# A decoder layer whose opening loads are reordered: part of the weights is fetched behind the first batch's opening, and SyncE and DVE take over loading work from GpSimd

## The chip, the cores and the metric

The kernel runs on one core of one Trainium2 chip. Its time is the device time of one execution in microseconds; lower is better. Kernels are compared by the median of several runs. One execution is taken with the hardware profiler, and all traces below come from such executions.

The core has five engines, each with a program of its own that it executes in order: TensorE (PE; its weight loads are listed apart as PEld), VectorE (DVE), ScalarE (ACT), GpSimd (POOL) and SyncE (SP). They wait for each other by semaphores. Transfers between the chip's main memory and the on-chip memory (SBUF) are issued by an engine's queue, here SyncE's and GpSimd's, and carried out by 16 DMA engines that all queues share. Matmul results are written to PSUM, whose buffers are few.

## The reference

One post-norm decoder layer in float32, batch 4, 1024 tokens of 256 features, a context of 154 tokens:

```python
x = _layernorm(x + self_attention(x))
x = _layernorm(x + cross_attention(x, ctx, distances))
x = _layernorm(x + mixture_of_experts(x))
```

The self attention has three parts. The first has 16 heads of 16 features, and its scores are scaled by a gate before the softmax:

```python
mod = sigmoid(x @ cg_W + cg_b + (cons_vec @ am_W + am_b))
scores = (q @ k.T / sqrt(16)) * mod[..., None]
```

Two further attentions of 4 heads of 64 features follow ("causal" on `x`, "meta" on the mix of the two), each mixed in by a constant weight, and an output projection. The cross attention adds `-log(distances + 1e-9) * abs(distance_scaling)` to its scores, where `distances` is 4 x 1024 x 154. The last part routes each token to 2 of 8 experts and adds a shared expert.

## The kernel before

**Stages.** Tokens lie on 128 partitions, 8 tiles of 128 to a batch. The four batches run one after the other through both attentions; then all 4096 tokens are routed, sent to their experts through a table in main memory (`scratch`), and put together again. `scratch` has 9216 rows of 258 numbers and is filled with zeros and with default row numbers at the start of the kernel by two transfers, `scratch<-empty` (9.4 MB) and `scratch<-rows` (9216 pieces of 8 bytes), lines 255 to 261. It is used again only after the attentions.

**The opening of a batch** is the generator `begin(b)`. It transposes the tokens on PE (`xT`, copied out by ACT), projects the gate (`project_mod`: PE, a Tanh on ACT, an affine step on POOL), `q` (PE, then DVE, which needs the gate and the bias `bq`) and `k` (PE, then ACT, which needs `bk`). Then come 12 steps of `maxima` (the lead): PE computes a 128 x 1024 block of scores (L422) into one of two large PSUM buffers, and DVE takes its maxima (L429). Between them lie the value projections of the first attention (L302, then DVE L310), and behind them the 8 tiles of the causal attention's values. For batches 1 to 3 `begin` runs step by step inside the batch before; for batch 0 it runs alone at the start.

**The main loop** has 128 steps for each batch. A step does one `maxima`, 12 steps ahead, and one `exponentials`: PE makes a block of scores (L460) into small PSUM buffers (three, and one accumulator), and ACT turns each half into exponentials (L471). Every fourth step's exponentials are multiplied with the values (L480). At steps 4, 8 and 12 the gate, `q` and `k` of the next group of heads are projected (L288).

**Loads.** The weights are loaded before `begin(0)` in the order of the text. `load_plain` issues one transfer from SyncE. `load_head_cols` loads a 256 x 256 matrix into a staging tile by SyncE; POOL fills a wider tile with zeros and copies the 16 heads' columns into it, at a distance of 32. `load_head_bias` issues four tiny transfers from POOL into a tile that DVE has filled; `load_cols` and `load_bcast` issue one each from POOL. The staging tiles share ten buffers (tag `ex`) with the exponentials, and `empty` and `rows` share theirs with later tiles of the tags `avq` and `rb`.

**What sets the order.** The text is written in one sequence. A scheduler distributes it over the engines and may place an instruction earlier or later in an engine's program where data allow; what it placed is what each engine executes. So the logarithm over `bias` (the distances of a batch, line 942: ACT, then a multiply by `nds` on DVE, line 943), written far behind the main loop, stands among the first instructions of ACT and DVE for batch 0. `nds` is the negated scaling, loaded at line 248 and finished by two small DVE operations (L250, L251). `cabout` and `mcbout` are biases that DVE scales after they are loaded (L230).

SyncE's transfers use eight semaphores in turn, and so do POOL's: an issue waits until the transfer issued eight places before it on the same engine has landed.

The transfers of `bias` and `cn` (the context) of a batch are issued at the head of the batch's loop (lines 816 and 818), for batch 0 just ahead of `begin(0)` and, in the order of SyncE's queue, ahead of the two fills of `scratch`.

Of the kernel before, what the change touches and what calls it, by code (L numbers as in the profile page):

```python
# [8 lines left out]
F32 = mybir.dt.float32  # L9
# [31 lines left out]
def run(gen):  # L41
    for _ in gen:
        pass
# [3 lines left out]
def decoder_layer(ctx: ExitStack, tc: tile.TileContext, a, out):  # L47
# [85 lines left out]
    with tc.tile_pool(name="wA", bufs=1) as wA, tc.tile_pool(name="work", bufs=2) as work:  # L133


        def load_plain(name, src, n):
            t = wA.tile([P, src.shape[0] // P, n], F32, tag=name, name=name)
            nc.sync.dma_start(t, src.rearrange("(c p) n -> p c n", p=P))
            return t

        def load_head_cols(name, src):

            st = work.tile([P, NC2, H], F32, tag="ex", name="stage", bufs=EXB)
            nc.sync.dma_start(st, src.rearrange("(c p) n -> p c n", p=P))
            t = wA.tile([P, NC2, NH, 32], F32, tag=name, name=name)
            nc.gpsimd.memset(t, 0.0)
            for c in range(NC2):
                nc.gpsimd.tensor_copy(
                    t[:, c, :, 0:HD], st[:, c, :].rearrange("p (h d) -> p h d", d=HD)
                )  # L150
            return t.rearrange("p c h w -> p c (h w)")

        def load_head_bias(name, src, extra):

            t = wA.tile([P, NG], F32, tag=name, name=name)
            if extra == 0.0:
                nc.vector.memset(t, 0.0)
            else:
                tmp = work.tile([P, NG], F32, tag="tmpb", name="tmpb")
                nc.vector.memset(tmp, extra)  # L160
                nc.vector.tensor_scalar(t, tmp, rowmx, None, ALU.mult)
            v = src.rearrange("(g j d) -> j d g", j=4, d=HD)
            for j in range(4):
                nc.gpsimd.dma_start(t[32 * j : 32 * j + HD, :], v[j])
            return t

        def load_cols(name, src):
            t = wA.tile([P, src.shape[0] // P], F32, tag=name, name=name)
            nc.gpsimd.dma_start(t, src.rearrange("(c p) -> p c", p=P))
            return t  # L170

        def load_bcast(name, src):
            t = wA.tile([P, H], F32, tag=name, name=name)
            nc.gpsimd.dma_start(t, src.unsqueeze(0).to_broadcast([P, H]))
            return t


# [60 lines left out]
        xwq = load_head_cols("xwq", a["xWqT"])  # L238
        xbq = load_head_bias("xbq", a["L0_xattn_bq"], 0.0)
        xwk = load_head_cols("xwk", a["xWkT"])  # L240
        xbk = load_head_bias("xbk", a["L0_xattn_bk"], 0.0)
        xwv = load_plain("xwv", a["xWvT"], H)
        xbv = load_bcast("xbv", a["L0_xattn_bv"])
        xwo = load_plain("xwo", a["xWoT"], H)
        xbo = load_bcast("xbo", a["L0_xattn_bo"])

        nds = wA.tile([P, 1], F32, tag="nds", name="nds")
        nc.gpsimd.dma_start(nds, a["ds"].to_broadcast([P, 1]))
        nds2 = work.tile([P, 1], F32, tag="nds2", name="nds2", bufs=1)
        nc.vector.tensor_scalar(nds2, nds, -1.0, None, ALU.mult)  # L250
        nc.vector.tensor_tensor(nds, nds, nds2, ALU.min)  # L251


        empty = work.tile([P, H], F32, tag="avq", name="empty", bufs=3)
        nc.gpsimd.memset(empty, 0.0)
        rows = work.tile([P, TILES, 2], F32, tag="rb", name="rows", bufs=1)
        nc.gpsimd.memset(rows, 0.0)
        iota(rows[:, :, 0], [[P, TILES]], 2 * B * S, 1)
        sv = scratch.rearrange("(t p) w -> p t w", p=P)
        nc.sync.dma_start(sv[:, :, 0:H], empty.unsqueeze(1).to_broadcast([P, TILES, H]))  # L260
        nc.sync.dma_start(sv[:, :, H:RW], rows)


        def ex_tile(shape, name):
# [512 lines left out]
        def end(b, cx4):  # L777
# [28 lines left out]
            if b < B - 2:  # L806

                nc.sync.dma_start(kept[b].rearrange("(t p) d -> p t d", p=P), y)
                load_y(b + 2)

        behind = iter(())
        for b in range(B):
            y = ys[b]
# [525 lines left out]
```

## Time and profile before

| | us |
|---|---|
| median of 6 runs | 3434.39 |
| lowest and highest run | 3430.82 and 3438.36 |
| the profiled execution | 3439.73 |
| its span (first to last instruction) | 3437.9 |

The mean granted clock of TensorE in the profiled execution was 0.974 of full speed.

The profile's rows read as follows. In the timeline: start in us from the beginning of the span, duration, engine, line of the kernel, operation, `output<-input` by the program's names, shapes, count (x), and in brackets the idle time of the engine just before and what ended it. "SPq" is an issue by SyncE's queue: its duration is that of the issue, not of the transfer. A float32 matmul of the program appears as two rows. In the table of stretches each row holds the busy time of the five engines, the number of instructions, the granted clock of PE (1.00 is full speed), the share of the DMA engines in use and what they moved.

Some durations of the opening that are used below:

| what | us |
|---|---|
| projection of 128 x 1024 (L288, 8 rows) at full clock | 3.60 to 3.70 for 8 rows, 4 matmuls |
| one DVE maximum (L429) | 1.22 to 1.24 |
| one lead step of scores and values at half clock | 4.02 |
| 16 value matmuls of the causal attention (L302, 32 rows) | 8.69 |
| exponentials of half a block (L471) | 0.60 |
| ACT's Ln over `bias` (L942) | 1.32 |
| ACT's table load | 1.28 |
| SyncE issues at the start, from one to the next | 0.49 to 0.62 |

### The profile page before, as it was taken

The numbers are of one execution on the slowest core, as the hardware profiler recorded it, in microseconds if no ns is written. First come the engines' busy times: TensorE is split into PE (matmuls) and PEld (weight loads), VectorE is DVE, ScalarE is ACT, GpSimd is POOL, SyncE is SP. The second block draws the span as 40 slices with busy tenths as digits, with TensorE's granted clock in tenths as the row PEclk, the third lists the DMA queues.
The fourth block names the chain that finished last, engine by engine and source line by source line (L and its number), as shares of the span: only waits on it lengthen the run. The fifth ranks groups of instructions, "written<-read, shape, count | busy, mean of one in ns | idle before, by whom it ended". The sixth has DMA issues, their size and how long they took to land.

```text
span 3437.9 us, 60936 instructions
## 1 busy us (share of the span) xinstructions
PE 3305.1 (96%) x25260; PEld 2086.4 (61%) x25260; DVE 1725.6 (50%) x3571; ACT 1600.8 (47%) x3130; POOL 373.4 (11%) x601
## 2 busy tenths in 40 slices
PE   7999999999999999999999999999999999999997
PEld 4555667566556675665566656555667665555554
DVE  3565555565655555656555556565556541122224
ACT  1555545375555344755564447555544731222223
POOL 4000000000000000000000000000000018212123
PEclk7999999999999999999999999999999999999999
DMA  9000000000000000000000000000000052111114
GB/s 203 1 2 1 1 1 1 3 21 14 1 1 1 1 1 3 21 13 2 1 1 1 1 3 9 1 2 1 1 1 1 1 204 82 44 44 44 44 44 156
DMA packets 75866, 84.13 MB, mean 24 GB/s; under 512 B 15136, under 2 KB 65928, under 8 KB 75592
## 3 DMA queue, kind: packets, MB, share of 16 engines
q1 hardware_dynamic: 68040, 61.53, 6.6%
q0 software_dynamic: 7552, 18.70, 1.6%
q8 instruction: 202, 3.31, 0.4%
q14 instruction: 72, 0.59, 0.1%
HBM read 46.52 MB, written 33.69 MB: 23 GB/s over the span
## 4 chain that ended last, share of the span: by engine, by line
PE 81%; DVE 9%; POOL 3%; issue 3%; ACT 2%; DMA 2%; SPq 0%; ACTq 0%; DVEq 0%; POOLq 0%
PE big L288 10%; PE big L422 8%; PE big L530 8%; PE one L566 7%; PE acc L584 7%; PE big L1226 7%; PE one L480 7%; DVE mxp L429 6%; PE one L460 4%; PE acc L1248 4%; PE one L697 3%; PE big L662 3%; PE one L302 2%; PE acc L716 2%; PE big L630 2%
## 5 line engine op out<-in xcount | busy, mean ns | idle before, releaser
L429 DVE TENSOR_REDUCE mxp<-big 128x2 f32<-128x1024 f32 x512 | 610.5, 1219 | 304.9 <-PE acc L460 252.2
L422 PE MATMUL big<-k,q 31*128 31x512 f32 x2048 | 596.0, 644 | 30.3 <-DVE mxp L429 26.7
L471 ACT ACTIVATE ex<-one 128x512 f32<-128x512 f32 x696 | 391.3, 601 | 248.5 <-PE acc L460 184.3
L460 PE MATMUL one<-q,k 32*128 32x256 f32 x2784 | 502.0, 397 | 0.0
L269 DVE CUSTOM_DVE_ANT_0 prob<-big,zero_t 128x1024 f32<-128x1024 f32 x256 | 303.6, 1222 | 270.8 <-PE big L530 270.6
L460 PEld LDWEIGHTS one<-q,k 32*128 32x128 f32 x2784 | 326.9, 185 | 31.1 <-ACT ex L471 2.5
L549 ACT ACTIVATE prob<-prob,nmx 128x1024 f32<-128x1024 f32 x256 | 293.0, 1153 | 22.2 <-DVE nmx L269 21.6
L530 PE MATMUL big<-mk,mq 64*128 64x512 f32 x1024 | 283.0, 630 | 2.4 <-ACT ex L468 2.4
L422 PEld LDWEIGHTS big<-k,q 31*128 31x128 f32 x2048 | 179.9, 189 | 172.1 <-DVE mxp L429 93.7
L571 ACT COPY pt<-one 128x512 f32<-128x512 f32 x256 | 137.6, 588 | 307.9 <-PE one L566 307.9
L566 PEld LDWEIGHTS one<-ident,prob 128*128 128x128 f32 x2048 | 220.8, 142 | 97.2 <-issue 91.5
L1226 PE MATMUL big<-wall,xt 128*128 x576 | 273.6, 598 | 1.8 <-POOL by L1202 1.8
L460 PE MATMUL acc<-q,k 32*128 32x256 f32 x928 | 263.9, 403 | 0.0
L566 PE MATMUL one<-ident,prob 128*128 128x128 f32 x2048 | 256.6, 279 | 0.0
L480 PE MATMUL one<-ex,v 128*32 128x256 f32 x4096 | 249.2, 383 | 0.0
L1236 DVE TENSOR_TENSOR hidr<-big,slr 128x512 f32<-128x512 f32 x72 | 49.8, 691 | 334.6 <-ACT slr L1234 334.6
L682 ACT ACTIVATE xs<-xs,xmx 128x154 f32<-128x154 f32 x512 | 174.5, 414 | 70.4 <-DVE xmx L269 70.3
L480 PEld LDWEIGHTS one<-ex,v 128*32 128x32 f32 x4096 | 119.8, 110 | 123.5 <-ACT ex L471 35.8
L573 DVE COPY pt<-one 128x512 f32<-128x512 f32 x256 | 164.4, 684 | 10.0 <-PE one L566 10.0
L269 DVE CUSTOM_DVE_ANT_0 xs<-big,bias 128x154 f32<-128x154 f32 x512 | 132.1, 314 | 67.3 <-ACT avx L724 33.5
L530 PEld LDWEIGHTS big<-mk,mq 64*128 64x128 f32 x1024 | 99.4, 190 | 100.7 <-issue 78.9
L460 PEld LDWEIGHTS acc<-q,k 32*128 32x128 f32 x928 | 155.2, 185 | 0.0
(266 smaller groups left out, 4721.6 us busy)
## 6 DMA issues: line engine op xcount, KB each, us to landing
xg<-scratch SPq DMA_DIRECT2D x72, 129.0 KB
scratch<-empty SPq DMA_DIRECT2D x1, 9216.0 KB
r<-result SPq DMA_DIRECT2D x8, 1024.0 KB
y<-in_x_dram SPq DMA_DIRECT2D x4, 1024.0 KB
wall<-in_L_ffn_w_gate_dram SPq DMA_DIRECT2D x8, 512.0 KB
wall<-in_L_ffn_w_up_dram SPq DMA_DIRECT2D x8, 512.0 KB
wall<-in_L_ffn_w_down_dram SPq DMA_DIRECT2D x8, 512.0 KB
bias<-in_fside_BxSxS_dram SPq DMA_DIRECT2D x4, 616.0 KB
```

The lines of the kernel that those rows point to most:

```text
L269: nc.vector.tensor_tensor_reduce(out=out, in0=ps, in1=bias, scale=-1.0, scalar=3.0e38, op0=ALU.add, op1=ALU.min, accum_out=low,)
L288: nc.tensor.matmul(ps[:, tb, :], w[:, c, lo : lo + P], xT[:, c, tb * 512 : (tb + 1) * 512], start=(c == 0), stop=(c == NC2 - 1),)
L422: nc.tensor.matmul(ps[:, jj, :], st["q"][r : r + MR, tok : tok + P], st["k"][r : r + MR, kb * 512 : (kb + 1) * 512], start=True, stop=True,)
L429: nc.vector.reduce_max(mxp[:, t, kb, 2 * pair : 2 * pair + 2], ps, axis=AX.X)
L460: nc.tensor.matmul(scs[jj][:, i * QW : (i + 1) * QW], st["k"][r : r + MR + 1, kc * P : (kc + 1) * P], st["q"][r : r + MR + 1, part * QW : ...
L471: nc.scalar.activation(ex[:, jj, :], scs[jj], AF.Exp, scale=1.0 / HD**0.5)
L480: nc.tensor.matmul(av[32 * j : 32 * j + 32, 0:QW], self.v[:, kc, h * VW : h * VW + 32], exs[kc // 2, j // 2][:, j % 2, i : i + QW], start= ...
L530: nc.tensor.matmul(pss[i][:, kb, :], q[r : r + MD, t * P : (t + 1) * P], k[r : r + MD, kb * 512 : (kb + 1) * 512], start=True, stop=True,)
L549: nc.scalar.activation(p, p, AF.Exp, bias=nmx[:, i : i + 1], scale=-1.0, accum_out=sm[:, t % 4, i : i + 1],)
L566: nc.tensor.transpose(ps[:, kc * P : (kc + 1) * P], probs[u][i][:, at : at + P], ident)
L584: nc.tensor.matmul(av[64 * i : 64 * i + 64, (t % 4) * P : (t % 4 + 1) * P], v[:, kc, h * MD : (h + 1) * MD], flipped[u][i][:, kc, :], star ...
L1226: nc.tensor.matmul(ps[:, g, :], xt[:, c * P : (c + 1) * P], wall[:, bass.ds(off + (g * NC2 + c) * D, D)], start=(c == 0), stop=(c == NC2 - 1),
```

## The change

Three things change in the text.

- The weight loads that `begin(0)` does not use (`gw`, the meta attention, `wo`, all of the cross attention, `nds`), the load of batch 1's tokens and the two fills of `scratch` move from ahead of `begin(0)` to behind it. `run(begin(0))` itself moves from inside the batch loop to just ahead of them, and so stands ahead of batch 0's transfers of `bias` and `cn` too.
- `load_head_cols` takes the engine that pads: DVE for `wq` and `wk`, POOL as before for `xwq` and `xwk`.
- The small loads (`load_head_bias`, `load_cols`, `load_bcast`, `nds`) are issued by SyncE instead of POOL.

```diff
-        def load_head_cols(name, src):
+        def load_head_cols(name, src, eng):
             st = work.tile([P, NC2, H], F32, tag="ex", name="stage", bufs=EXB)
             nc.sync.dma_start(st, src.rearrange("(c p) n -> p c n", p=P))
             t = wA.tile([P, NC2, NH, 32], F32, tag=name, name=name)
-            nc.gpsimd.memset(t, 0.0)
+            eng.memset(t, 0.0)
             for c in range(NC2):
-                nc.gpsimd.tensor_copy(
+                eng.tensor_copy(
                     t[:, c, :, 0:HD], st[:, c, :].rearrange("p (h d) -> p h d", d=HD)
                 )
...
             for j in range(4):
-                nc.gpsimd.dma_start(t[32 * j : 32 * j + HD, :], v[j])
+                nc.sync.dma_start(t[32 * j : 32 * j + HD, :], v[j])
...
         def load_cols(name, src):
-            nc.gpsimd.dma_start(t, src.rearrange("(c p) -> p c", p=P))
+            nc.sync.dma_start(t, src.rearrange("(c p) -> p c", p=P))
...
         def load_bcast(name, src):
-            nc.gpsimd.dma_start(t, src.unsqueeze(0).to_broadcast([P, H]))
+            nc.sync.dma_start(t, src.unsqueeze(0).to_broadcast([P, H]))
...
-        nc.sync.dma_start(gw, a["L0_ffn_gate_w"].rearrange("(c p) e -> p c e", p=P))
-        wq = load_head_cols("wq", a["L0_attn_Wq"])
+        wq = load_head_cols("wq", a["L0_attn_Wq"], nc.vector)
...
-        wk = load_head_cols("wk", a["L0_attn_Wk"])
+        wk = load_head_cols("wk", a["L0_attn_Wk"], nc.vector)
...
         ca = load_mha("ca", CAUSAL_W)
-        load_y(1)
-        mc = load_mha("mc", META_W)
-        wo = load_plain("wo", a["L0_attn_Wo"], H)
         bo = load_bcast("bo", a["L0_attn_bo"])
...
+        run(begin(0))
+
+        load_y(1)
+        nc.sync.dma_start(gw, a["L0_ffn_gate_w"].rearrange("(c p) e -> p c e", p=P))
+        mc = load_mha("mc", META_W)
+        wo = load_plain("wo", a["L0_attn_Wo"], H)
+        xwq = load_head_cols("xwq", a["xWqT"], nc.gpsimd)
+        xbq = load_head_bias("xbq", a["L0_xattn_bq"], 0.0)
+        xwk = load_head_cols("xwk", a["xWkT"], nc.gpsimd)
+        xbk = load_head_bias("xbk", a["L0_xattn_bk"], 0.0)
+        xwv = load_plain("xwv", a["xWvT"], H)
+        xbv = load_bcast("xbv", a["L0_xattn_bv"])
+        xwo = load_plain("xwo", a["xWoT"], H)
+        xbo = load_bcast("xbo", a["L0_xattn_bo"])
...
+        nc.sync.dma_start(nds, a["ds"].to_broadcast([P, 1]))
...
+        nc.sync.dma_start(sv[:, :, 0:H], empty.unsqueeze(1).to_broadcast([P, TILES, H]))
+        nc.sync.dma_start(sv[:, :, H:RW], rows)
+
         behind = iter(())
         for b in range(B):
...
             nc.sync.dma_start(cn, a["ctx_1024"][b].rearrange("(c p) d -> p c d", p=HK))
 
-            if b == 0:
-                run(begin(0))
             sa, xT, v64 = begun[b]
```

In the changed text the two operations over `bias` stand at lines 944 and 945, and the fills of `scratch` at 812 and 813.

More of the change, by code (lines that the diff above doesn't have):

```diff
@@ L233, in decoder_layer @@
         ca = load_mha("ca", CAUSAL_W)
-        load_y(1)
-        mc = load_mha("mc", META_W)
-        wo = load_plain("wo", a["L0_attn_Wo"], H)
         bo = load_bcast("bo", a["L0_attn_bo"])
[L238 to L261, printed above, removed]
         def ex_tile(shape, name):
@@ L809, in end @@
                 load_y(b + 2)
+        run(begin(0))
[11 more added lines that the diff above has]
+        xbo = load_bcast("xbo", a["L0_xattn_bo"])
+        nds = wA.tile([P, 1], F32, tag="nds", name="nds")
+        nc.sync.dma_start(nds, a["ds"].to_broadcast([P, 1]))
+        nds2 = work.tile([P, 1], F32, tag="nds2", name="nds2", bufs=1)
+        nc.vector.tensor_scalar(nds2, nds, -1.0, None, ALU.mult)
+        nc.vector.tensor_tensor(nds, nds, nds2, ALU.min)
+        empty = work.tile([P, H], F32, tag="avq", name="empty", bufs=3)
+        nc.gpsimd.memset(empty, 0.0)
+        rows = work.tile([P, TILES, 2], F32, tag="rb", name="rows", bufs=1)
+        nc.gpsimd.memset(rows, 0.0)
+        iota(rows[:, :, 0], [[P, TILES]], 2 * B * S, 1)
+        sv = scratch.rearrange("(t p) w -> p t w", p=P)
+        nc.sync.dma_start(sv[:, :, 0:H], empty.unsqueeze(1).to_broadcast([P, TILES, H]))
+        nc.sync.dma_start(sv[:, :, H:RW], rows)
         behind = iter(())
```

## The prediction

> **What bounds the kernel now.** The page first: PE is busy nearly all the time, and only the first of the 40 slices shows a poor clock.
>
> ```profile
> span 3437.9 us, 60936 instructions
> PE 3305.1 (96%) x25260; PEld 2086.4 (61%) x25260; DVE 1725.6 (50%) x3571; ACT 1600.8 (47%) x3130; POOL 373.4 (11%) x601
> PEclk7999999999999999999999999999999999999999
> ```
>
> The change touches only the start, so the table of short stretches comes next (per stretch: busy us of PE, PEld, DVE, ACT, POOL, then granted clock, DMA share, GB/s).
>
> ```profile
> 25.00:30.00 5.00, 2.06 (x7) 0.95 (x5) 0.76 (x1) 1.46 (x2) 4.45 (x10) 1.00 0.47 119
> 30.00:35.00 5.00, 0.00 (x0) 0.00 (x0) 0.75 (x2) 2.15 (x2) 4.91 (x8) 0.72 0.59 169
> ...
> 55.00:69.00 14.00, 13.45 (x34) 5.16 (x30) 7.29 (x9) 0.00 (x0) 0.00 (x0) 0.50 1.20 228
> 69.00:73.00 4.00, 4.00 (x11) 2.52 (x8) 1.65 (x2) 0.00 (x0) 0.00 (x0) 0.50 1.87 10
> 73.00:74.00 1.00, 1.00 (x6) 0.88 (x5) 0.42 (x1) 0.00 (x0) 0.00 (x0) 0.94 1.83 7
> ```
>
> PE stands still from 27 to 37 us; in one-us stretches the clock then falls to half at 32.4 and stays there until 73.05. The timeline says why PE stood, and what the queues held:
>
> ```profile
> 28.54 1.32 ACT L942 ACTIVATE bias<-bias,tiny_t 128x1232 f32<-128x1232 f32 x1 [8.06 <-DMA bias<-in_fside_BxSxS_dram]
> 31.83 0.37 SPq L260 DMA_DIRECT2D scratch<-empty  x1
> 34.11 27.81 SPq L261 DMA_DIRECT2D scratch<-rows  x1
> 34.22 0.15 DVE L250 TENSOR_SCALAR nds<-nds 128x1 f32<-128x1 f32 x1 [6.95 <-DMA nds<-in_ds_dram]
> 36.96 2.08 PE L302 MATMUL one<-wv,xT 128*128 128x256 f32 x4 [9.90 <-DVE v L310]
> 38.97 2.09 PE L422 MATMUL big<-k,q 31*128 31x512 f32 x8
> ...
> 82.26 1.73 ACT L471 ACTIVATE ex<-one 128x512 f32<-128x512 f32 x3 [0.39 <-PE one L460]
> ```
>
> PE's 9.90 us were a wait for DVE, and DVE stood for `nds`, the last of POOL's loads. The other thing to see is SyncE: the 9.4 MB write of `scratch` goes out at 31.83, and the issue behind it (`rows`) takes 27.81 us. `bias` was fetched before both.
>
> **What the change moves.** In the built programs PE's order is the same, matmul for matmul, from within the lead on, and ACT's from its 16th instruction; DVE's last moved row is the `bias` multiply. So the price is how far one point behind all that shifts. I take the first maximum of step 5 of the main loop, a PE L422 at 90.31 in this trace.
>
> *Removed.* POOL issues no load any more, and the first `q` waits only for `x`, `wq`, `bq` and `mod`. `x` lands as before (first transpose 6.57). The small loads for the gate's bias now wait on SyncE, the last issued at about 7.2, landing at about 9.5; the 4-matmul group (1.86 us) and 5 transposes (1.30) end at about 13, the second copy of xT (1.01) at 14.2, three projections of 1.8 each (3.60 a row pair) at 19.7, k's ACTIVATE (1.09) at about 21. The lead's scores begin near 21 instead of 38.97. PE then has no gap over 4 us, so the clock should hold; the lead and `v64`, 39.6 us at half clock (38.97 to 78.55), then take about 30: 8 steps of 2.0 (half of 4.02), four maxima at DVE's 1.24, 16 value tiles at 0.54 (8.69 us for 16 on record, mostly at full clock). The first exponentials come near 51 instead of 79.81. That is 28 us, if nothing else is late. DVE's own padding (two memsets, four copies, under 1.1 us each by POOL's 0.94 and 0.37 a copy) lies in DVE's idle 6 us before 8.26 and between loads; it costs nothing while `stage` (about 7 us) is what is waited for, about 1 us otherwise.
>
> *Added: `bias` goes behind `scratch`.* ACT's program now runs k, three steps of exponentials, a table load, the Ln over `bias` (its line 944), a table load, then the fourth step's exponentials. ACT executes in that order: everything behind stands until `bias` lands. SyncE issues 49 loads (20 of its own, 29 taken from POOL) before `scratch`, then `rows`, then `bias`.
>
> Issue of `scratch`: 49 starts at 0.50 (the first rows of SyncE stand 0.49 to 0.62 apart) = 24.5, from 0.74. Every issue also waits for the load eight places before it: the trace has this as SyncE's wait of 1.5 us before `cn` for `mcwin`, eight issues earlier. Laid out with 0.35 MB/us and 2.3 us from issue to landing (y: first bytes 1.3 us after issue, about 0.95 from last byte to use), these waits are 1.5 (for `x`), 1.6 (bk, for DVE's fill), 0.6, 2.2 (for y1), 1.6 (`mcwin`), 0.3: 7.8 in all. Sum 33.0, against 31.83 before. Ends: 31 (issue 0.42, 0.37 MB/us) to 39 (each at the 0.72 of POOL's first issue).
>
> From there to the end of `rows`: 31.83 to the last small packets in 82 to 83, so 50.9 us. Ends: 46 (the whole write nearer the 333 GB/s of its first ten us than its mean of 253) to 54 (at 240 throughout, with the loads' tail ahead of it). That the queue serves in order is read from packet sizes: of the 9216 8-byte packets of `rows` none is seen from 34 to 60, 132 up to 66, 1589 from 66 to 69. `bias` follows: 0.63 MB at 0.3 MB/us is 2.1, and 0.95 to its use, 3.0. Landing at 33.0 + 50.9 + 3.0 = 86.9. The lead is done at 51 (at half clock 61), so ACT waits some 25 to 35 us and all of the 28 us gained are inside that wait.
>
> Then Ln 1.32 and table load 1.28 with 0.1 of gaps: the fourth step's first exponential at 89.6. In this trace it is the third of the group at 82.26, at 83.4. That is +6.2. While it waits PE can run on to the gate's projection (3.69) but not past it: the next transposes need a PSUM buffer that this exponential frees. After it come 1.65 us of exponentials and the 16 L480 products, 1.86 us, or 3.7 at half clock: step 5 at +5.35 instead of +6.9, a gain of 1.55. The clock will be at half there, PE having been idle for over 4 us. At 1472.6 it fell and was back at 1479.4 with the loop's own mix; at 342.9 for 3.4 us. I take 5 us of dense work until it is back, and 0.8 us lost in step 5 beyond the 1.85 counted. Queued behind ACT are PE (products), DVE (maxima, behind its own `bias` multiply of 1.25, in the same wait) and POOL; nothing else is late, as `cn` is not needed before 600 us.
>
> The Trainium skill ("ScalarE: Activation LUTs", section on what ACT_TABLE_LOAD costs) gives a switch of table 1.28 us and 1.38 of drain besides. The trace has the load at 635.64, 1.28 long, and the next ACTIVATE at 636.93, with no drain behind it; by the page the sum would be about 1.4 more.
>
> The clock at a restart: this trace has PE 95% busy from 37 to 69 at 0.50. The skill ("TensorE: Matmul & The Clock Gate", Part 1) says that about 3.4 us of sustained work release the throttle; the row contradicts it for that mix, and by the page alone the half-clock terms (1.85 + 0.8) would shrink to about 1.
>
> *Sum*: +6.2 - 1.55 + 0.8 = **+5.5 us**. The profiled execution took 3439.73 (span 3437.9), so it would be 3445.2; the median of the six runs is 3434.39, 5.3 lower, so **3439.9**. 0.2% (6.9 us) is about what a measurement of this kernel can tell from no change; the forecast is a loss just inside it.
>
> **Rivals.**
> A. *`bias` is not held up by the queue.* If the engines mix `bias` with what is queued, SyncE still cannot issue it before `rows` is issued, at about 33.0 + 2.3 + 27.8 = 63; landing at about 68, 19 earlier: 3439.9 - 19 = 3421. Were ACT not to wait at all, the full 28: 3406. For: the 28 us are plainly there. Against: the packet sizes. Chance 0.13.
> B. *The clock sticks.* At the restart PE stays at half clock as it did for 40.6 us at the start. Half of that, less the fifth of the chain there that is DVE's maxima (20.6% from 83 to 130 us), is +16: 3456. It decides once the low clock outlasts about 7 us. For: the start. Against: at 346, 1479 and 2170 the loop's mix brought it back in 3.4 to 6.8 us; the lead's L422 fills 31 rows at a time. Chance 0.10.
> C. *SyncE is slower at the small loads than at its own.* At POOL's 0.72 each `scratch` goes out at 39: +6, 3446; at the 1.1 that its issues take when the queue is full, later still. This is the upper end of the forecast's case, with a chance of 0.15 in its 0.72.
> The rest, 0.05, is an unlisted wait at the start of either sign.
>
> **How the numbers follow.** The forecast's case (0.72) has `scratch` at 31 to 39, the drain 46 to 54, the clock 1 to 7 us: most of it -5 to +13, that is 3429 to 3447, with its middle at 3440. The range reaches down into A and up towards B: 3426 to 3452. Over 0.2% slower: B and somewhat under half of the forecast's case, 0.42; within 0.2%: the rest of that case and of the unlisted, 0.43; faster: A and a little, 0.15.
>
> **What would show it.** Right: L422 begins near 21 us; `scratch` is issued at about 33; ACT's Ln over `bias` stands at about 87 with an idle time of some 30 us before it, ended by the DMA of `bias`; PE is idle from about 57 to 89 and its clock at half behind it; then the trace is the old one, shifted by about 5 us. Wrong: Ln before 75 (A); a clock of 0.50 beyond 100 us (B); issues over 0.6 us apart (C); or a shift that grows behind 110 us, which no step here explains.

## The result and the profile after

| | before | after |
|---|---|---|
| median, us | 3434.03 (43 runs) | 3444.05 (21 runs) |
| lowest and highest run | 3430.52 to 3441.94 | 3437.62 to 3455.01 |
| the profiled execution | 3439.73 | 3440.36 |
| its span | 3437.9 | 3438.5 |

The ratio is 1.0031, with a 95% interval of 1.0024 to 1.0038: the change costs 10.0 us (8 to 13). The forecast was a loss of 5.5 us, to 3439.9, with a range of 3426 to 3452. The sign was right, the size was not quite.

The two profiled executions differ by 0.6 us only. Before's profile is a long execution among its runs, after's a short one among its own, so the two must be compared place by place. The page of after first, with the rows that the prediction showed of before:

```profile
span 3438.5 us, 60917 instructions
PE 3288.9 (96%) x25260; PEld 2079.6 (60%) x25260; DVE 1725.4 (50%) x3577; ACT 1600.7 (47%) x3130; POOL 353.5 (10%) x566
PEclk8999999999999999999999999999999999999999
```

PE is as busy as before (96%), and again only the first slice has a poor clock. POOL has 35 instructions fewer, most of them loads that SyncE now issues. What the opening looks like, from the timeline (start, duration, engine, line, operation, count, idle time before and what ended it):

```profile
24.79 1.14 PE L394 MATMUL big<-k,q 31*128 31x512 f32 x8
...
33.82 0.38 SPq L812 DMA_DIRECT2D scratch<-empty  x1
34.30 29.31 SPq L813 DMA_DIRECT2D scratch<-rows  x1
...
54.92 1.57 ACT L443 ACTIVATE ex<-one 128x512 f32<-128x512 f32 x3 [30.20 <-PE one L432]
...
58.48 1.28 ACT L944 ACT_TABLE_LOAD   x1
59.71 3.70 PE L260 MATMUL big<-xT,cgw 128*128 128x512 f32 x8
63.66 19.49 SPq L820 DMA_DIRECT2D bias<-in_fside_BxSxS_dram  x1
...
89.00 1.32 ACT L944 ACTIVATE bias<-bias,tiny_t 128x1232 f32<-128x1232 f32 x1 [29.25 <-DMA bias<-in_fside_BxSxS_dram]
...
91.64 0.60 ACT L443 ACTIVATE ex<-one 128x512 f32<-128x512 f32 x1
92.29 0.69 PE L315 MATMUL one<-ident,mxcol 128*128 128x128 f32 x2 [28.88 <-ACT ex L443]
93.27 3.26 PE L452 MATMUL one<-ex,v 128*32 128x256 f32 x32 [0.29 <-ACT ex L443]
96.46 0.70 PE L394 MATMUL big<-k,q 31*128 31x512 f32 x2
```

The scores of the lead (L394, L422 before) begin at 24.79 instead of 38.97 and the first exponentials at 54.92 instead of 79.81. Then ACT stands at the Ln (L944) for 29.25 us until `bias` has landed, because SyncE issued `bias` behind both fills of `scratch`. PE gets as far as the gate's projection (L260) and stands for 28.88 us. Step 5 of the main loop, the prediction's landmark, begins at 96.46 (the last row) instead of 90.31: +6.15 us.

The stretches of the lead's end and around the wait (busy us of PE, PEld, DVE, ACT, POOL, then granted clock, DMA share, GB/s):

```profile
45.00:50.00 5.00, 5.00 (x18) 4.16 (x17) 2.50 (x4) 0.00 (x0) 0.00 (x0) 0.68 1.13 243
...
60.00:65.00 5.00, 3.41 (x8) 1.14 (x7) 0.00 (x0) 0.00 (x0) 0.00 (x0) 1.00 1.14 239
65.00:70.00 5.00, 0.00 (x0) 0.00 (x0) 0.00 (x0) 0.00 (x0) 0.00 (x0) 0.87 1.21 215
70.00:75.00 5.00, 0.00 (x0) 0.00 (x0) 0.00 (x0) 0.00 (x0) 0.00 (x0) 0.50 1.88 19
75.00:80.00 5.00, 0.00 (x0) 0.00 (x0) 0.00 (x0) 0.00 (x0) 0.00 (x0) 0.50 1.74 5
...
85.00:90.00 5.00, 0.00 (x0) 0.00 (x0) 0.00 (x0) 0.99 (x1) 0.00 (x0) 0.50 0.66 154
90.00:95.00 5.00, 2.42 (x22) 1.10 (x26) 2.42 (x3) 4.67 (x7) 0.21 (x1) 0.50 0.00 0
95.00:100.00 5.00, 4.55 (x56) 2.74 (x48) 2.35 (x2) 2.44 (x5) 0.83 (x1) 0.90 0.00 0
```

All compute engines are idle while the DMA engines write out first the 9.4 MB (over 200 GB/s until about 69) and then the 8-byte pieces of `rows` (5 GB/s from 75 to 80, at a DMA share of 1.74), and last fetch `bias`. The clock is full until some 5 us after PE's last matmul (63.4), then half; work begins again at 92.3 and the clock is full again at 96. The first row shows a shorter spell in the lead: from 44.81 to 48.22 the clock was at half although PE worked without a pause.

### The profile page after: what moved, and what is told of

It reads as the page before. It is cut to its first block, busy times and chain, and to the rows that moved or that the text cites. A ratio compares the mean times of both kernels' runs of the same rounds, so it can differ in the third digit from the quotient of the medians.

```text
span 3438.5 us, 60917 instructions
## 1 busy us (share of the span) xinstructions
PE 3288.9 (96%) x25260; PEld 2079.6 (60%) x25260; DVE 1725.4 (50%) x3577; ACT 1600.7 (47%) x3130; POOL 353.5 (10%) x566
## 4 chain that ended last, share of the span: by engine, by line
PE 80%; DVE 9%; issue 3%; DMA 3%; ACT 2%; POOL 2%; SPq 1%; ACTq 0%; DVEq 0%; POOLq 0%
PE big L260 10%; PE big L502 8%; PE one L538 7%; PE big L394 7%; PE acc L556 7%; PE big L1228 7%; PE one L452 7%; DVE mxp L401 6%; PE one L432 4%; PE acc L1250 4%; PE one L669 3%; PE big L634 3%; PE acc L688 2%; PE big L602 2%; PE one L274 1%
## 5 line engine op out<-in xcount | busy, mean ns | idle before, releaser
L394 PE MATMUL big<-k,q 31*128 31x512 f32 x2048 | 586.4, 632 | 29.2 <-DVE mxp L401 25.6
L502 PE MATMUL big<-mk,mq 64*128 64x512 f32 x1024 | 284.7, 634 | 2.4 <-ACT ex L440 2.4
L394 PEld LDWEIGHTS big<-k,q 31*128 31x128 f32 x2048 | 177.4, 186 | 165.8 <-DVE mxp L401 86.4
L452 PE MATMUL one<-ex,v 128*32 128x256 f32 x4096 | 249.7, 384 | 0.3 <-ACT ex L443 0.3
L452 PEld LDWEIGHTS one<-ex,v 128*32 128x32 f32 x4096 | 120.0, 110 | 123.5 <-ACT ex L443 36.5
L502 PEld LDWEIGHTS big<-mk,mq 64*128 64x128 f32 x1024 | 99.7, 191 | 101.8 <-issue 80.0
```

Of the source, the lines that this page charges most:

```text
L394: nc.tensor.matmul(ps[:, jj, :], st["q"][r : r + MR, tok : tok + P], st["k"][r : r + MR, kb * 512 : (kb + 1) * 512], start=True, stop=True,)
L452: nc.tensor.matmul(av[32 * j : 32 * j + 32, 0:QW], self.v[:, kc, h * VW : h * VW + 32], exs[kc // 2, j // 2][:, j % 2, i : i + QW], start= ...
L502: nc.tensor.matmul(pss[i][:, kb, :], q[r : r + MD, t * P : (t + 1) * P], k[r : r + MD, kb * 512 : (kb + 1) * 512], start=True, stop=True,)
```

## The experiments

Nine variants ran besides the two kernels. "Step 5" is the start of the first score matmul behind the first L452 group, in the profiled execution. The shift of the median is taken against the kernel before in the same series of runs.

| kernel | step 5 | against before's 90.31 | median | shift of the median |
|---|---|---|---|---|
| changed kernel | 96.46 | +6.2 | 3444.05 | +10.0 |
| e1_bias_first | 66.22 | -24.1 | 3415.65 | -19.9 |
| e2_rows_last | 83.81 | -6.5 | 3425.59 | -10.0 |
| e4_order_only | 85.05 | -5.3 | 3434.07 | -1.5 |
| e5_engines_only | 103.52 | +13.2 | 3449.40 | +13.9 |
| e6_fills_late | 68.49 | -21.8 | 3414.79 | -19.6 |
| e7_kept_warm | 96.28 | +6.0 | 3446.60 | +12.2 |
| e8_other_queue | 75.19 | -15.1 | 3420.76 | -12.0 |
| e9_fills_in_loop | 64.68 | -25.6 | 3412.15 | -20.6 |
| e10_warm_longer | 92.99 | +2.7 | 3440.07 | +7.4 |

### `bias` ahead of the fills

The first batch's transfers of `bias` and `cn` are put in the text just ahead of the fills.

```diff
+        def load_batch(b):
+            bias = work.tile([P, NT, S2], F32, tag="bias", name="bias", bufs=1)
+            nc.sync.dma_start(bias, a["fside_BxSxS2_0"][b].rearrange("(t p) k -> p t k", p=P))
...
+        first = load_batch(0)
         empty = work.tile([P, H], F32, tag="avq", name="empty", bufs=3)
...
+            bias, cn = first if b == 0 else load_batch(b)
```

> Edit: the changed kernel, but batch 0's transfers of bias and cn are issued by SyncE just ahead of the two fills of scratch instead of behind them. Theory (ACT's Ln waits for bias, and bias waits for the fills): Ln runs near 39 us while the lead is still going, the first exponentials come at 55 us as in the changed kernel, step 5 starts near 65 us (90.3 before, 96.5 in the changed kernel), and the whole is 25 us faster than before, about 3409. Rival (the loss is the clock or the slower issue of small loads on SyncE): step 5 stays near 90 or the time stays at 3430 to 3445.

Measured: 3415.65, ratio 0.9942 (0.9929 to 0.9955). The timeline of this kernel:

```profile
32.21 0.43 SPq L808 DMA_DIRECT2D bias<-in_fside_BxSxS_dram  x1
...
33.31 0.90 SPq L820 DMA_DIRECT2D scratch<-empty  x1
...
39.14 1.32 ACT L949 ACTIVATE bias<-bias,tiny_t 128x1232 f32<-128x1232 f32 x1 [12.56 <-DMA bias<-in_fside_BxSxS_dram]
...
55.72 1.57 ACT L443 ACTIVATE ex<-one 128x512 f32<-128x512 f32 x3 [13.96 <-PE one L432]
```

`bias` is used 6.9 us behind its issue instead of 25.3 (63.66 to 89.00), while ACT has nothing else to do, and the exponentials wait for PE alone. Step 5 moves by 24.1 us against before and by 30.2 against the changed kernel. The opening is the expected one (Ln near 39, exponentials at 55, step 5 near 65); the median is not, 3409 was expected. So the opening's gain was there, as rival A's full-gain variant had it, and the place of one load in the queue took all of it and 6 us more.

### One fill ahead of `bias`, the other behind

```diff
         nc.sync.dma_start(sv[:, :, 0:H], empty.unsqueeze(1).to_broadcast([P, TILES, H]))
-        nc.sync.dma_start(sv[:, :, H:RW], rows)
+        first = load_batch(0)
+        nc.sync.dma_start(sv[:, :, H:RW], rows)
```

> Edit: the changed kernel, but only the second fill of scratch (rows, 9216 pieces of 8 bytes) is issued behind bias and cn; the 9.4 MB fill stays ahead of them. It sizes the two parts of the wait. Theory: the rows fill is worth 10 to 13 us of the wait on the slowest ring, so Ln starts near 77 us instead of 89, step 5 near 84, and the time is about 12 us below the changed kernel's 3444, near 3432. Rival (the engines mix what is queued): Ln does not move and the time stays at 3444.

Measured: 3425.59, ratio 0.9969 (0.9957 to 0.9981). Timeline:

```profile
31.90 0.38 SPq L812 DMA_DIRECT2D scratch<-empty  x1
32.33 32.24 SPq L815 DMA_DIRECT2D bias<-in_fside_BxSxS_dram  x1
...
68.33 1.43 SPq L821 DMA_DIRECT2D scratch<-rows  x1
75.98 1.32 ACT L949 ACTIVATE bias<-bias,tiny_t 128x1232 f32<-128x1232 f32 x1 [16.69 <-DMA bias<-in_fside_BxSxS_dram]
```

Now the issue of `bias` itself takes 32.24 us: whatever SyncE issues next behind the 9.4 MB is held. From the issue of `empty` to the Ln are 44.1 us here and 55.2 in the changed kernel. The 9216 pieces of 8 bytes, 0.07 MB in all, are thus worth 11 us of the wait (7 to 13 over all executions with that order, 50.7 to 57.5 us) and the 9.4 MB the rest. Ln and step 5 came as expected (near 77 and 84), the median 6 us lower than the 3432 expected.

### Each half of the change alone

The reorder alone (the changed kernel, but POOL pads `wq` and `wk` and issues the small loads), and the change of engines alone (the kernel before with its own order, DVE and SyncE doing that work):

```diff
-                nc.sync.dma_start(t[32 * j : 32 * j + HD, :], v[j])
+                nc.gpsimd.dma_start(t[32 * j : 32 * j + HD, :], v[j])
...
-        wq = load_head_cols("wq", a["L0_attn_Wq"], nc.vector)
+        wq = load_head_cols("wq", a["L0_attn_Wq"], nc.gpsimd)
```

> Edit: the changed kernel, but POOL pads wq and wk and issues the small loads, as before; only the order of the text is changed. In its program SyncE issues bias ahead of the fills again. Theory: Ln runs near 30 us; POOL's late loads now stall DVE inside the lead (mcbout until about 33 us, nds until about 45 us), PE idles and falls to half clock, first exponentials near 70 to 79 us (79.8 before): 0 to 10 us faster than before, 3424 to 3434. Rival (moving begin(0) ahead is by itself what delays bias): Ln near 85 us, time near 3444.

> Edit: the kernel before, but DVE pads wq and wk and SyncE issues the small loads; the order of the text is as before. In its program the fills go ahead of bias, and Ln stands ahead of the first exponentials. Theory: bias lands near 89 us as in the changed kernel, the first exponentials come near 92 us (79.8 before), and the time is 10 to 14 us above before, 3444 to 3448, so that this half of the change holds the whole loss. Rival (the loss comes from the reordering): 3434 or less.

Measured: the reorder alone 3434.07, ratio 0.9996 (0.9987 to 1.0005), no change that can be told; the engines alone 3449.40, ratio 1.0045 (1.0033 to 1.0057). Timeline and stretches of the reorder alone:

```profile
28.04 1.32 ACT L944 ACTIVATE bias<-bias,tiny_t 128x1232 f32<-128x1232 f32 x1 [1.33 <-DMA bias<-in_fside_BxSxS_dram]
...
35.17 0.17 DVE L229 TENSOR_SCALAR mcbout<-mcbout 128x2 f32<-128x2 f32 x1 [6.92 <-DMA mcbout<-in_L_attn_mc_bout_dram]
...
36.52 2.08 PE L394 MATMUL big<-k,q 31*128 31x512 f32 x4 [5.95 <-DVE mxp L401]
...
42.33 0.37 SPq L812 DMA_DIRECT2D scratch<-empty  x1
```

```profile
30.00:35.00 5.00, 0.57 (x3) 0.10 (x1) 0.00 (x0) 0.67 (x1) 4.99 (x9) 0.53 0.18 27
...
50.00:68.00 18.00, 17.45 (x40) 7.90 (x39) 8.94 (x11) 0.00 (x0) 0.00 (x0) 0.50 1.09 262
```

`bias` is early here, and the lead starts at 25.86. But POOL issues the loads late (`mcbout` at 32.40), DVE's scaling of `mcbout` stands between its maxima, and PE waits 5.95 us for DVE (30.57 to 36.52). The clock falls to half at 30.3, just ahead of that wait, and stays there until 67.8, with PE busy for 17.45 of 18 us from 50 on; the first exponentials come at 74.55. So the wait costs its 5.95 us, but that it put the clock down is not shown, nor that the clock would have come back sooner without it. The kernel before had the same wait with `nds` in the place of `mcbout`; there the clock fell some 5 us into it.

The engines alone, timeline:

```profile
32.39 0.38 SPq L260 DMA_DIRECT2D scratch<-empty  x1
32.87 30.03 SPq L261 DMA_DIRECT2D scratch<-rows  x1
62.95 18.00 SPq L816 DMA_DIRECT2D bias<-in_fside_BxSxS_dram  x1
...
88.98 1.32 ACT L942 ACTIVATE bias<-bias,tiny_t 128x1232 f32<-128x1232 f32 x1 [55.92 <-DMA bias<-in_fside_BxSxS_dram]
...
92.27 2.30 PE L460 MATMUL one<-q,k 32*128 32x256 f32 x8 [21.49 <-ACT ex L471]
```

In the text of this kernel the fills stand ahead of `bias`, exactly as in the kernel before, which issues `bias` at 16.20 all the same. There the scheduler had put `bias` first since the fills' source tiles came late: POOL, busy with small loads, filled `empty` at 31.48 and `rows` at 31.72 and 33.86. With the loads gone from POOL the tiles are ready early (iota into `rows` at 12.04 with the engines alone, 12.29 in the changed kernel), the fills go out as soon as SyncE reaches them, and `bias` stands behind. So it is the change of engines, not the move of `begin(0)`, that puts the fills ahead of `bias`. That the scheduler's reason is this readiness is argued from the built programs, and the padding and the small loads were not moved apart; that the order comes with this half of the change is what the runs show. The half alone is dearer than the whole (+13.9 against +10.0), since in its program the Ln stands ahead of all exponentials: PE goes on at the same time as in the changed kernel (92.27 and 92.29), but with most of the first four steps and the gate's projection still to do (last row).

### The fills later

Two variants. In the first the fills stand in the text behind the twelfth step of the first main loop, with source tiles of their own.

```diff
+                if b == 0 and n == 12:
+                    empty = work.tile([P, H], F32, tag="empty", name="empty", bufs=1)
+                    nc.gpsimd.memset(empty, 0.0)
...
+                    nc.sync.dma_start(sv[:, :, 0:H], empty.unsqueeze(1).to_broadcast([P, TILES, H]))
```

> bias and cn of the first batch ahead of the two fills of scratch, as in the run that had bias first (3415.65), and the fills issued later still: in program order behind the twelfth step of the first batch's main loop, with tiles of their own for their source. If the fills' traffic beside the lead costs that run something (its clock was 0.66 from 45 to 50 us and the loads behind it share the engines with the write), step 5 comes 1 to 4 us earlier than its 66 us and the median is 3411 to 3414. If a write of 9.4 MB costs nothing to what runs beside it, 3415 to 3416. If the write, now beside the loop, takes bandwidth or clock there, 3418 or more.

Measured: 3414.79, ratio 0.9935 (0.9922 to 0.9947). It does not answer its question: SyncE issued the fills at 33.56, right behind `bias` and `cn`, since nothing in the data kept them back. It is the first experiment with other tiles, and repeats its result. In the second the source tiles are made from the first batch's attention times zero:

```diff
+                nc.gpsimd.tensor_scalar(empty, ctok[:, 0, :], 0.0, None, ALU.mult)
...
+                    rows.rearrange("p t w -> p (t w)"), ctok[:, 0, 0 : 2 * TILES], 0.0, None, ALU.mult
```

> bias and cn of the first batch first, and the fills of scratch really late: their source tiles are made from a tile of the first batch's attention times zero, so the fills go out some 500 us or more into the program (in the run called e6_fills_late SyncE still issued them at 33.56). If the write of 9.4 MB beside the lead costs the lead nothing, step 5 stands at 66 to 69 as in e1 and e6 and the median at 3412 to 3418. If it takes something there, step 5 comes earlier than 65 and the median is under 3412. If the write costs the loop it now lies beside, the median is over 3418.

Measured: 3412.15, ratio 0.9939 (0.9926 to 0.9953). `rows` goes out at 218 us and `empty` at 287, earlier than the expectation's 500, but well behind the opening. Step 5 stands at 64.68 against 66.22 and 68.49, between the two cases of the expectation. Two differences of the openings account for most of that: in e6_fills_late the lead begins later (the `cgw` projection ahead of it starts at 15.34 and not at 11.88), and in e1_bias_first the clock was at half from 46.1 to 49.5 in the lead, which takes 1.7 us, while e6_fills_late and e9_fills_in_loop had no such spell. The ratios of the three kernels agree within their intervals (some 4 us to either side). So no cost of the write of 9.4 MB beside the lead or beside the loop can be told; what it costs is what stands behind it in its queue.

### `bias` through another queue

The order of the changed kernel stays, but POOL issues `bias`, held until `nds` has landed so that the fills are out first.

```diff
-            nc.sync.dma_start(bias, a["fside_BxSxS2_0"][b].rearrange("(t p) k -> p t k", p=P))
+            eng = nc.gpsimd if b == 0 else nc.sync
+            if b == 0:
+                nc.gpsimd.tensor_copy(bias[:, 0, 0:1], nds)
+            eng.dma_start(bias, a["fside_BxSxS2_0"][b].rearrange("(t p) k -> p t k", p=P))
```

> The changed kernel, with the first batch's bias fetched through POOL's queue instead of SyncE's. A one-column copy of nds into bias on POOL ahead of the load keeps that load behind nds, so that it goes out at about 36 to 40 us, some 3 us or more behind the first fill of scratch. The program then has the Ln ahead of the first exponentials on ACT. Theory Q, bias was late because it stood behind the fills in the same queue: it lands 3 to 7 us after its issue, Ln at 40 to 48, first exponentials near 55 as in the changed kernel, step 5 at 66 to 69 and a median of 3414 to 3418. Theory S, the 9.4 MB that are handed out keep the DMA engines busy for whatever comes later, on any queue: Ln at 70 to 89, step 5 at 80 to 98, median 3428 to 3446.

Measured: 3420.76, ratio 0.9965 (0.9952 to 0.9977). Timeline:

```profile
32.03 1.73 SPq L812 DMA_DIRECT2D scratch<-empty  x1
33.85 28.45 SPq L813 DMA_DIRECT2D scratch<-rows  x1
...
37.27 1.13 POOL L823 DMA_DIRECT2D bias<-in_fside_BxSxS_dram  x1 [0.32 <-POOL bias L822]
...
48.05 1.28 ACT L947 ACT_TABLE_LOAD   x1 [23.21 <-DMA bias<-in_fside_BxSxS_dram]
49.35 1.32 ACT L947 ACTIVATE bias<-bias,tiny_t 128x1232 f32<-128x1232 f32 x1
50.70 0.86 DVE L948 TENSOR_SCALAR bias<-bias,nds 128x1232 f32<-128x1232 f32 x1 [7.90 <-ACT bias L947]
52.75 2.08 PE L394 MATMUL big<-k,q 31*128 31x512 f32 x4 [8.46 <-DVE mxp L401]
```

Issued 5.2 us behind the fill, `bias` is there 10.8 us later (37.27 to 48.05), while the fill is being written. It is neither free (e1_bias_first: 6.9 us to the Ln) nor held to the end of the fill: theory Q, with a longer flight than its 3 to 7 us. Ln, step 5 (75.19) and the median all lie between the ranges of the two theories, nearer to Q. The 16 DMA engines serve both queues; within SyncE's queue the order of issue holds. The rest of the gain is missing because DVE's multiply over `bias` stands among its maxima in this program: DVE waited 7.90 us for the Ln, PE with both large buffers full waited 8.46 us for DVE, and the clock was at half from 45 to 59.

The Trainium skill ("DMA: Bandwidth & Descriptors", section "Queues, rings and completion order") says that a DMA engine takes turns, packet by packet, between the queues that have work, and works through one queue's descriptors in their order. Both halves agree with these rows. The same page's section "Issuing engines are not separate DMA queues" says that starting transfers on several engines saves only the issuing engine's time, usually small beside the transfer. Here it moved the use of `bias` from 89.00 to 49.35, and the issue was not small: on SyncE it ended at 83.15, on POOL at 38.40. So behind a long transfer "usually small" does not hold.

### The clock at the restart

The gate's projection ahead of the wait is computed several times over, to keep PE busy.

```diff
-            for tb in range(2):
+            for tb in list(range(2)) * times:
```

> The second call of the gate's projection (PE's L260 ahead of the wait for bias) is computed eight times over, to the same values, so that PE is busy for 3.7 x 8 = 29.6 us, from 59.7 to about 89, instead of standing from 63.4 to 92.3. Nothing else is changed. If the restart at half clock costs what the trace shows (L315 and L452, 3.95 us at 0.50, half of which is lost, and nothing behind 96), step 5's first L394 stands at about 94.5 instead of 96.46, and the median is 1 to 3 us under the changed kernel's 3444. If the long group of runs is a clock that stays low after the wait (theory C), that group is gone and the median falls to about 3438. If the long group comes from the write of scratch (W) or from the loop (L), the two groups stay, each 2 us lower.

Measured, eight times over: 3446.60, ratio 1.0034 (1.0021 to 1.0046), like the changed kernel. Timeline:

```profile
58.92 27.73 PE L262 MATMUL big<-xT,cgw 128*128 128x512 f32 x64
91.73 0.69 PE L317 MATMUL one<-ident,mxcol 128*128 128x128 f32 x2 [5.08 <-ACT ex L446]
...
92.71 3.64 PE L455 MATMUL one<-ex,v 128*32 128x256 f32 x32 [0.29 <-ACT ex L446]
```

The expectation failed: 64 rows took 27.73 us and not 29.6, PE stood for 5.08 us instead of 28.88, and that was enough. The clock fell 4.3 us after the last matmul and stayed at half for 6.8. So with nine:

> The gate's projection ahead of the wait nine times over, to the same values. With eight, a call took 3.49 us and not 3.7, PE's work ended at 86.65, and the clock fell 4.3 us later, at 91, for the 6.7 us it also stays low elsewhere; so that run did not take the low clock away. With nine, PE's work ends at about 90.1, 1.6 us ahead of the restart. If idling over 4 us is what lowers the clock, it now stays at 1.00, L452 of the fourth step takes 1.93 and not 3.26 to 3.64, step 5 stands at 94.0 to 94.8 and the median is 1 to 3 us below the changed kernel's 3444. If the clock falls in spite of it, step 5 stays at 96 to 97.8.

Measured: 3440.07, ratio 1.0027 (1.0014 to 1.0040). Timeline:

```profile
59.81 31.17 PE L262 MATMUL big<-xT,cgw 128*128 128x512 f32 x72
90.82 0.38 PE L317 MATMUL one<-ident,mxcol 128*128 128x128 f32 x2
91.13 1.93 PE L455 MATMUL one<-ex,v 128*32 128x256 f32 x32
```

No idle time ahead of the restart and no low clock there (this execution had its own short spell at half earlier, from 45.0 to 48.4, with PE at work): the 32 rows of L455 take 1.93 us instead of 3.26 to 3.64. That is the price of the restart at half clock, 1.3 to 1.7 us there and 0.3 in the transposes ahead of it (0.38 instead of 0.69). The earlier step 5, 92.99, comes mostly from `bias`, which in this execution was used at 84.62 already; PE's extra work held step 5 back by some 2.9 us (ACT's exponentials began at 87.26, so PE could have gone on at 87.9 as it did 0.65 us behind them in the changed kernel, but its repeats ended at 90.8). The runs of this kernel still spread from 3433.78 to 3456.73, so it is not the restart that spreads them. The interval overlaps that of the changed kernel; that the median is lower is not shown.

### Where the other 4 us are

The changed kernel was profiled twice more, and the kernel before once.

> The changed kernel once more, for a second look at an execution. Its times come in two groups, about 3438 to 3444 and 3448 to 3455, and the first profile was one of the short group (Ln over bias at 89.0, step 5's first L394 at 96.46, clock back at 96). If this execution is a long one (about 3450): theory W, that the write of scratch takes longer in it, wants the Ln at 94 to 100 and everything behind shifted by as much; theory C, that the clock stays at half after the restart, wants the Ln near 89 and a clock of 0.50 beyond 100 us, step 5 long; theory L, that the opening is alike and the loop behind it loses more clock, wants step 5 within 1 us of 96.5 and a shift that grows behind 110 us. If it is a short one, all three want the first profile again, step 5 within 1 us of 96.5.

> The changed kernel a third time, for the same reason and with the same readings: Ln at 94 to 100 in a long execution by theory W, near 89 with 0.50 beyond 100 us by theory C, step 5 near 96.5 and a growing shift by theory L; the first profile again in a short one.

> The kernel before, looked at once more. In the runs so far the median's shift is about 4 us more than the shift of step 5 between the profiles (changed kernel +10.0 against +6.15, bias first -19.9 against -24.1, fills in the loop -20.6 against -25.6). Either the first profile of the kernel before, at 3439.7 and 5 us over its median, had a late opening: then this one, if it is near 3434, has step 5 at 85 to 88 and not at 90.31. Or its opening was the usual one and its loop lost more clock than usual (64 us of clock behind 100 us in that profile): then step 5 stands at 89.5 to 91.5 and the loop loses about 59.

| execution | time | Ln over `bias` | step 5 | span behind step 5 | clock lost behind 100 us |
|---|---|---|---|---|---|
| before, first | 3439.73 | 28.54 | 90.31 | 3347.6 | 64.2 |
| before, again (b2_again) | 3436.95 | 28.61 | 89.78 | 3345.4 | 62.5 |
| after, first | 3440.36 | 89.00 | 96.46 | 3342.0 | 59.5 |
| after, again (a2_again) | 3440.75 | 88.50 | 96.33 | 3342.7 | 58.5 |
| after, again (a3_again) | 3451.08 | 89.92 | 97.76 | 3351.5 | 68.4 |

The last column is the sum, over stretches of 10 us from 100 to 3430, of 10 us times one minus the granted clock. a3_again is a long execution. Its opening is 1.4 us later than that of a2_again, its Ln stands at 89.92 and not at 94 or later, and its clock is back by 98: theories W and C fall. What is long in it is the rest: 8.8 us more, and 9.9 us more of clock lost, in short spells at half clock in the main loops (theory L). One of them in the timeline of a3_again:

```profile
1041.23 2.05 PE L432 MATMUL big<-q,k 32*128 32x256 f32 x16 [1.10 <-ACT ex L440]
1043.49 4.11 PE L502 MATMUL big<-mk,mq 64*128 64x512 f32 x8 [0.21 <-ACT ex L440]
```

and the same place in the timeline of a2_again, which got there 9.4 us earlier:

```profile
1031.82 2.05 PE L432 MATMUL big<-q,k 32*128 32x256 f32 x16 [1.10 <-ACT ex L440]
1034.08 2.96 PE L502 MATMUL big<-mk,mq 64*128 64x512 f32 x8 [0.21 <-ACT ex L440]
```

The same instructions, with the same 1.10 and 0.21 us of idle time ahead of them; in one execution the clock fell to half (0.71 at 1043, 0.50 from 1044 to 1046) and the eight rows of L502 took 1.15 us longer. Over all 14 profiled executions of the study the span behind step 5 lies between 3341.0 and 3352.9 us, whatever was done to the opening, and the kernel before lies inside it. The opening itself repeats: 89.78 and 90.31 before, 96.33 to 97.76 after, a shift of 6 to 8 us. The median of the changed kernel is loose besides: of its 21 times 11 lie from 3437.62 to 3444.05 and 10 from 3447.80 up, so the median is the last of the lower group, and one run changing sides would have made it 3447.80. So of the 10.0 us of the medians some 7 are the opening, and about 3 are left, by subtraction, for what lies behind it. The profiles do not show them: the mean span behind step 5 is 3346.5 us in the two profiles of before and 3345.4 in the three of after. b2_again settles its own question for the usual opening (89.78); its loops lost 62.5 us of clock, less than in the first profile but more than the 59 expected. Whether the change makes the low spells more frequent or these runs met more of them by chance is open. In the table of variants the median's shift lies 2 to 6 us above that of step 5 in eight of ten kernels, 0.7 above it in e5_engines_only and 3.5 below it in e2_rows_last.

## Why the prediction was nearly right, point by point

- **Where the gain of the opening goes.** Right. The forecast said that the 28 us gained end in ACT's wait for `bias`, with Ln at about 87 and some 30 us idle before it: 89.00 and 29.25. Putting `bias` ahead of the fills gave back 30.2 us at step 5 and 29.9 between the shifts of the medians (+10.0 and -19.9).
- **Start of the lead.** The mis-sized term. "Three projections of 1.8 each" should have been 3.6 each: 4 matmuls, 8 rows, take 3.60 in the trace of before as well, and after's three rows last 4.59, 3.60 and 3.60. The lead began at 24.79 and not near 21 (nor 5.4 us later than that, as the first projection started at 12.10 and not at 14.2). It cost nothing here, as ACT's wait covers it; it is the main reason why the uncovered gain in e1_bias_first is 24.1 us and not 28.
- **Length of the lead.** About 30 us at full clock was forecast; 24.79 to 54.92 is 30.1, but that is in part luck. The clock was at half from 44.81 to 48.22, though PE had no gap over 4 us and the forecast let it hold; without such a spell the lead takes 28.5 us (25.52 to 54.02 in a2_again, 25.69 to 54.19 in a3_again).
- **SyncE's issues.** 49 starts of 0.50 and 7.8 us of eight-place waits gave 33.0; 33.82 measured, and 31.8 to 34.0 in the other executions with the fills ahead of `bias` on SyncE. Rival C falls.
- **From the first fill to the Ln.** 50.9 to the end of `rows` and 3.0 for `bias` make 53.9; 55.2 measured, 56.4 to 57.5 in a2_again, a3_again, e5_engines_only and e7_kept_warm, 50.7 in e10_warm_longer. With the drain's ends of 46 to 54 this was 49 to 57, which holds nearly all of them.
- **From the Ln to step 5.** 2.7 and 5.35 were forecast, 2.64 and 4.82 measured. PE had run the gate's projection ahead, as the 1.55 us assumed, and the clock came back 3.7 us after the restart instead of 5 (5.8 and 4.7 in a2_again and a3_again). The sum was +4.65 to the start of step 5 and +0.8 within it. Measured were +6.15 at its start, +6.0 and +7.5 in the other two profiles, and in the first nothing within it, as the clock was back at 96.0: the late Ln and the spared 0.8 cancel in part.
- **Rival A** (`bias` not held by the queue): false in SyncE's queue, since `bias` was issued at 63.66, about where A had it, but used 25 us later. Largely true across queues, as e8_other_queue shows (10.8 us from the issue to the use).
- **Rival B** (the clock sticks): did not happen behind the wait. In the reorder alone the lead did run at half clock, from 30.3 to 67.8. ("95% busy from 37 to 69" in the kernel before is 93.5%: 29.93 of 32 us.)
- **"Then the trace is the old one, shifted".** This step failed. It took one execution's loops as fixed and corrected by the 5.3 us between before's profile and its median. The spans behind step 5 of one and the same kernel differ by up to 9.5 us between executions (3342.0 to 3351.5), more than the shift that was to be forecast. Of the 4.5 us between the forecast shift and that of the medians some 1.3 are the opening (6.8 on the mean of the profiles instead of 5.5) and some 3 are left for the spans behind it; no step of the prediction looked at that, and where they arise stays open.

## What to carry to other kernels

A load that becomes issuable earlier is a load that can get ahead of another: when work is taken from an engine, list what that engine's lateness was holding back, and see what the freed transfer now stands in front of. The bulk transfer of this kernel costs nothing that can be told beside the work, but everything behind it in its queue waits for it to drain, so the few hundred kilobytes that compute needs go ahead of it or through another queue. The best kernels of this study are the change with `bias` ahead of the fills (3412 to 3416, ratios 0.9935 to 0.9942), which beat both.

## What was not expected of the hardware

- An issue on SyncE behind the 9.4 MB fill lasted 27.5 to 32.5 us, in whichever transfer came next (`rows`, or `bias` in e2_rows_last), and the issue after `rows` another 15 to 20.
- 9216 pieces of 8 bytes hold up the next transfer for about 11 us (44.1 against 55.2 us from fill to Ln), though they are 0.07 MB.
- In the openings every spell at half clock lasted a whole number of steps of 3.41 us, read from stretches of 0.2 us: 3.41 (one step) in the leads of the changed kernel, e1_bias_first and e10_warm_longer, 6.82 (two) in e7_kept_warm, 13.65 (four) in e8_other_queue, 17.07 (five) in e2_rows_last, 27.31 (eight) in the changed kernel's wait, 37.54 (eleven) in e4_order_only and 40.96 (twelve) in the kernel before. The spell at 1043 us in a3_again is one step too.
- Where a step begins does not follow the work closely. In eight waits the clock fell 4.3 to 5.3 us after PE's last matmul, but 0.9 us after it in e8_other_queue, 1.7 in the second wait of e5_engines_only, and ahead of the wait in e4_order_only; behind the waits for `bias` it came back 3.7 to 6.1 us after the restart.
- A busy PE did not always bring it back: the lead ran at half for 26 to 36 us in the kernel before, e4_order_only and e5_engines_only, with PE 90 to 98% busy. In these three and in e8_other_queue it came back 3.2 to 4.1 us after the value matmuls of the causal attention began (69.86 and 73.12 in the kernel before), which fill 128 rows where the lead's score matmuls fill 31. That the rows are the reason is not tested.
- The Trainium skill ("TensorE: Matmul & The Clock Gate", Part 1) has an idle window of about 3.4 us lower the clock and about 3.4 us of sustained work raise it. The step of 3.41 us agrees with that and the restarts roughly (3.7 to 6.1 us); the leads at half clock and the spells with PE at work (44.81 in the changed kernel; 1043 us in a3_again, behind 1.3 us of idle time) do not.
